# Reordering the hand-written instruction list of a fused Mamba and mixture-of-experts kernel

## The chip, the core and the metric

The kernel runs on one core of one Trainium2 chip. The metric is the time of one execution in device microseconds (us); lower is better. One execution was also recorded by the hardware profiler, and its profile and trace are what the sections below read.

## What is computed

Two layers on x of 32 sequences x 256 tokens x 128 channels, all in fp32: a Mamba block and a mixture of experts, each behind a layer norm and added to x.

```python
# Mamba block, on xn = layernorm(x):  d_inner 256, d_state 16, dt_rank 8
xi, res = split(xn @ W_in)
u       = silu(causal_conv4(xi) + conv_b)
dr, B, C = split(u @ W_x)
delta   = softplus(dr @ W_dt + b_dt)
h_t     = exp(delta_t * A) * h_(t-1) + delta_t * B_t * u_t     # for 256 channels x 16 states
y_t     = sum over states of h_t * C_t, + u_t * D
x       = x + (y * silu(res)) @ W_out
# mixture of experts, on xn = layernorm(x): 8 experts, the 2 best per token
cw      = softmax over the two best of xn @ gate_w.T, zero elsewhere
x       = x + sum over e of cw[:, e] * (silu(xn @ w1[e].T) @ w2[e].T)
```

## The kernel before

**Tiling.** The 32 sequences are cut into 17 tiles (0 to 16): the first and the last hold one sequence, the fifteen others two. A tile's tokens stand as columns, its channels as the 128 partitions, in two chunks c. The 16 states of a chunk are taken in groups, so that every scan covers 128 x 1024 elements: four states at a time for a one-sequence tile (8 scans in all), two for the others (16). That makes 256 scans.

**The pieces.** The work is cut into small named pieces, each of which issues a few instructions. A word such as `1:sc3` means piece sc3 of tile 1. In the order in which a tile needs them:

- `ldx` (line L373) loads x; `st1*`, `sa1`, `rs1`, `ap1` are the layer norm (statistics on DVE L538, the power on POOL L554 to L557, the scaling on ACT L563); `tr1`, `hi1`, `nl1`, `lo1` transpose it on PE and split it into a high and a low part on ACT (L614, L624).
- `cv*` is the convolution with W_in folded in, on PE (L635); `u*` its silu (L649); `wx` the product pd with W_x (L658); `rh`, `sb`, `nr`, `rl` its evacuations on ACT (L685, L671, L695); `bcd` stores the B and C rows as bc in DRAM (L677); `gp*`, `gs*` are the gate; `zz`, `sp*` are delta (softplus, L739).
- For each scan k: `rb` and `rc` load B and C rows of bc, broadcast over all partitions (L778, 512 KB each, four buffers each); `dk` computes da = exp(delta A) on ACT (L760, nine buffers); `in` the product db = (delta u) B on DVE (L812); `sc` the scan h on DVE (L819, three buffers for h); `cm` the product h C on POOL (L830); `ys` adds it to y on PE (L834). A row is kept for two scans where the second chunk takes it up. `du`, `dp` (L793, L799) prepare delta u; in tile 0 `dq` does (L807).
- `yc`, `yz`, `yt`, `ye` gate and transpose y, `ldr` loads x once more, `px` and `op` add W_out's product on PE; `st2*` to `lo2` are the second norm.
- `gt`, `sc`, `r0` to `r4`, `rx`, `rw0` to `rw4` rank the experts. For each expert e: `wi` (two halves, three matmuls each, L1079), `si` their silu on ACT (L1092), `wo` on PE (L1100), `as` scales by cw on ACT (L1112), `aa` adds on POOL (L1118); `sto` stores the tile (L1141).

Before all that, pieces of tile 0 prepare weights: `lw`, `lc`, `ldk`, `ldp`, `ldd`, `ldo`, `ldg`, `l10`, `l11`, `ld2` load them (`ld2` is w2, 1 MB, L465), `pm`, `pt` make constants, `km`, `kh`, `kl` fold W_in into the convolution and split it, `ka` makes A, `kdt`, `kwr`, `kw`, `kgt`, `kdg` split or spread the others. In tile 0, `pb0` and `pc0` make the first B rows on PE and ACT instead of by a transfer.

**The order.** Nothing is scheduled by a compiler. One string, ORDER, lists all 3827 words, and the kernel issues them as they stand; each engine's queue, and the transfer queue SP's, takes its own instructions in that order, and waits where an operand or a buffer isn't ready:

```python
with tc.manual_schedule():
    for word in ORDER.split():
        i, n = word.split(":")
        pieces[n](int(i))
```

Two more things depend on the order. ACT holds one set of functions at a time, and a piece asks for its own (exp for `dk`, `ka`, `rx`; silu for `u`, `gs`, `si`; softplus for `sp`), so the order sets how many table loads (L530) there are:

```python
def need(which):
    if table[0] != which:
        nc.scalar.preload_act_table_set(SETS[which])
    table[0] = which
```

And a tile takes a buffer of its pool at the place in the order where its word stands, so a load waits for the last reader of the buffer that is free there.

Of the kernel before, what the change touches and what calls it, by code (L numbers as in the profile page):

```python
# [47 lines left out]
0:pm 0:ldx 0:lw0 0:lc0 0:lc1 0:ldk 0:lw1 1:ldx 0:ldg 0:st10 0:st11 0:l11 0:sa1 0:ldd 0:rs1 0:ldp 0:km0 0:ap1  # L48
3:ldx 0:tr1 0:l10 0:km1 0:hi1 0:nl1 0:kh1 0:lo1 0:kl1 0:kh0 0:cv1 0:kl0 1:st10 1:st12 1:st13 0:ka 1:st11 1:sa1
1:rs1 0:cv0 0:u1 1:ap1 0:kdt 2:ldx 1:tr1 0:u0 0:kwr 0:wx 0:gp0 0:sb 3:st10 0:rh 0:bcd 1:hi1 0:nr 0:ldo 0:rl  # L50
1:nl1 0:gs0 0:zz 1:lo1 0:pb0 0:kw0 0:sp0 1:cv0 0:pc0 0:rb1 0:rc0 0:rc1 2:st10 0:rb2 0:dq0 0:rb3 2:st13 0:in0
0:rc2 0:rc7 0:ld2 0:dk0 0:kw1 1:cv1 0:dk1 0:sc0 0:dk5 2:st12 0:cm0 0:in1 0:dk2 2:st11 2:sa1 0:sc1 0:dk4 0:kdg
0:rc3 2:rs1 0:ys0 0:dk3 0:in2 0:cm1 0:dk6 0:sc2 0:in3 0:cm2 1:u1 1:u0 3:st11 0:sc3 2:ap1 1:wx 0:ys1 0:dq1 1:rh
0:in6 1:sb 1:bcd 0:ys2 0:sc6 1:nr 1:gp0 1:gs0 1:rl 0:in4 1:zz 0:cm3 1:gp1 1:rb1 3:st13 0:sc4 1:rb5 1:sp0 0:ldr
1:sp1 0:pt 0:ys3 1:du0 0:in5 0:yc0 0:cm4 1:rb4 0:sc5 0:dk7 0:yz0 0:ys4 0:in7 0:kgt 1:dk3 0:cm6 0:yt0 1:dk0
1:rb0 0:sc7 2:tr1 1:rc1 0:px 1:dp0 0:cm5 1:rc0 2:hi1 1:dk6 1:dk2 0:cm7 0:ys5 1:in0 0:ys6 1:rb6 1:sc0 2:nl1
0:ys7 0:yc1 1:dk1 0:yz1 1:in1 1:du1 2:lo1 3:st12 1:rb2 0:ye0 3:sa1 0:yt1 4:ldx 1:cm0 1:sc1 0:ye1 1:rc2 1:dk4
0:op 1:dk8 1:cm1 2:gp0 0:st20 0:st21 1:dk5 1:ys0 1:in2 1:dk9 0:sa2 1:rb3 1:sc2 0:rs2 0:x2 1:rc4 1:rc3 1:rc5
0:ap2 0:tr2 1:in5 1:cm2 1:ys1 0:hi2 0:nl2 1:sc5 0:lo2 0:gt 0:wi50 1:gs1 2:gs0 0:sc 2:cv0 1:in3 0:si50 0:r3
1:rb7 1:sc3 0:r4 1:rc7 1:dk11 1:ys2 1:dk7 1:in4 1:cm3 0:rx 1:dk10 0:r0 1:sc4 1:dk12 3:rs1 1:rc6 1:ys3 0:wi40  # L60
1:in6 2:cv1 1:cm4 2:u0 4:st10 1:sc6 1:cm5 1:rc13 1:ys4 2:u1 0:r1 0:si40 2:wx 1:in7 3:ap1 0:wi00 0:r2 0:wi70
1:sc7 0:rw0 0:wi20 0:si70 1:ldr 0:rw4 1:ys5 2:rh 1:cm6 0:si00 1:dp1 2:gp1 0:si20 2:sb 0:wi41 1:in8 0:wi60
0:si60 1:cm7 2:gs1 3:tr1 1:rb15 1:sc8 0:wi71 2:nr 1:ys6 2:rl 0:si41 0:si71 0:wi11 3:hi1 1:in9 1:cm8 3:nl1
0:wi30 0:wi10 0:rw1 0:si10 1:rb13 1:sc9 0:si11 2:bcd 0:wi51 1:ys7 0:wi21 0:si21 1:in10 1:cm9 0:si51 0:wo7
0:si30 1:yc0 0:rw2 3:lo1 2:zz 1:rb12 1:sc10 1:rc11 0:wo2 1:ys8 1:dk15 1:in11 1:cm10 2:rb3 1:sc11 1:rc12 2:sp0
0:rw3 0:wo4 1:yz0 0:as2 2:sp1 0:wi01 0:as4 1:in12 1:ys9 0:aa4 0:wi31 4:st11 1:rb14 1:ys10 1:cm11 1:sc12 1:rc14
0:si01 1:yt0 0:wo0 1:dk13 1:in13 2:rc0 1:ys11 1:ye0 1:cm12 4:st12 2:rb0 1:dk14 1:sc13 2:dk2 1:rc15 1:ys12
1:in14 1:cm13 2:dk6 2:rb4 2:dk4 1:sc14 0:aa2 1:ys13 2:dk3 2:du0 1:in15 2:dk0 3:cv0 1:cm14 2:rb1 0:as7 1:sc15
2:rc3 2:dp0 0:as0 2:dk1 2:rc1 2:in0 1:cm15 2:dk7 4:st13 2:rb5 2:sc0 0:wi61 3:gp1 0:si31 1:ys14 2:in1 2:cm0
1:ys15 2:dk5 2:rb2 2:sc1 3:cv1 2:rc2 2:dk9 2:rc4 1:yc1 2:dk8 2:in3 2:cm1 2:ys0 4:sa1 2:sc3 2:du1 2:rc5 3:u1  # L70
2:rb6 3:u0 1:px 1:yz1 0:si61 2:in2 3:wx 5:ldx 2:cm3 1:yt1 2:sc2 2:ys1 1:ye1 3:rh 3:gp0 3:sb 3:gs0 2:rc6 2:in4
# [36 lines left out]
4:cm13 5:rb0 4:sc14 5:rc1 3:as1 4:ys12 3:as2 3:aa1 4:ys13 4:in15 6:lo1 5:dk1 4:px 4:cm14 7:st11 5:rb3 4:sc15
3:wo5 5:rc0 5:dp0 5:dk0 3:wo0 3:as5 5:in0 4:cm15 5:dk4 5:rb2 5:sc0 4:ys14 5:dk7 3:aa5 4:ys15 3:wo4 4:yc1 7:sa1
# [1117 lines left out]
```

## Time and profile before

| | |
|---|---|
| median of 3 runs | 1052.45 us (1048.10 to 1054.97) |
| profiled execution | 1053.02 us, of which its span is 1051.3 us |
| mean granted TensorE clock | 0.982 |
| read from HBM, written | 217.28 MB, 5.24 MB (212 GB/s over the span) |

Busy time of each engine in the three stretches that the first and the last scan bound (us; windows of the profile):

| stretch | length | PE | DVE | ACT | POOL |
|---|---|---|---|---|---|
| start to first scan, 0 to 28.16 | 28.16 | 18.61 | 12.32 | 17.85 | 6.45 |
| first to last scan, 28.16 to 1012.26 | 984.10 | 910.92 | 941.92 | 901.86 | 884.51 |
| last scan to end, 1012.26 to 1051.30 | 39.04 | 34.71 | 2.55 | 26.86 | 23.07 |

How to read the profile lines below. Engines: PE is the matmul engine, PEld its weight loads, DVE the vector engine, ACT the scalar engine, POOL the GpSimd engine, SP the queue that issues transfers. A group line gives the code line, engine, operation, output<-inputs with shapes and count | busy us, mean ns of one | idle us of the engine just before them, and what ended most of it. A timeline line gives start us, duration us, and the instruction, and in brackets the idle time before it and who ended it. A wait line gives total us, times, longest. A window line gives the stretch, then busy us and instructions for PE, PEld, DVE, ACT, POOL, then the granted clock of PE, the DMA share and GB/s. The slices are 40 equal parts of the span, each digit the busy share in tenths.

### The profile page before, as it was taken

The numbers are of one execution on the slowest core, as the hardware profiler recorded it, in microseconds if no ns is written. First come the engines' busy times: TensorE is split into PE (matmuls) and PEld (weight loads), VectorE is DVE, ScalarE is ACT, GpSimd is POOL, SyncE is SP. The second block draws the span as 40 slices with busy tenths as digits, with TensorE's granted clock in tenths as the row PEclk, the third lists the DMA queues.
The fourth block names the chain that finished last, engine by engine and source line by source line (L and its number), as shares of the span: only waits on it lengthen the run. The fifth ranks groups of instructions, "written<-read, shape, count | busy, mean of one in ns | idle before, by whom it ended". The sixth has DMA issues, their size and how long they took to land.

```text
span 1051.3 us, 18971 instructions
## 1 busy us (share of the span) xinstructions
PE 964.2 (92%) x6757; PEld 843.7 (80%) x6757; DVE 956.8 (91%) x903; ACT 946.6 (90%) x1914; POOL 914.0 (87%) x688
## 2 busy tenths in 40 slices
PE   6578789999999999999999999999899999999998
PEld 4467667979888887978888887978778888887898
DVE  3999999999999999999999999999999999999950
ACT  6867989999899998999999898989989998899977
POOL 2577788979989999989999999998989999899975
PEclk9879999999999999999999999999999999999999
DMA  5565848658486775758577684848667584776500
GB/s 180 192 225 173 282 149 281 238 183 275 159 249 220 243 268 192 265 165 283 194 263 247 197 284 140 285 176 282 231 215 252 191 286 159 256 233 201 172 11 17
DMA packets 86095, 223.75 MB, mean 213 GB/s; under 512 B 8049, under 2 KB 35313, under 8 KB 85873
## 3 DMA queue, kind: packets, MB, share of 16 engines
q1 hardware_dynamic: 86000, 222.55, 63.7%
q8 instruction: 53, 0.87, 0.3%
q14 instruction: 42, 0.34, 0.1%
HBM read 217.28 MB, written 5.24 MB: 212 GB/s over the span
## 4 chain that ended last, share of the span: by engine, by line
PE 34%; ACT 29%; DVE 18%; POOL 10%; issue 7%; DMA 1%; SPq 0%; DVEq 0%; POOLq 0%; ACTq 0%
DVE h L819 11%; ACT da L760 11%; PE pf L1079 10%; PE y L834 7%; POOL h L830 6%; PE pe L1100 6%; DVE db L812 6%; ACT L530 5%; ACT so L1112 4%; ACT hs L1092 3%; PE pc L635 3%; POOL x L1118 2%; PE po L941 1%; PE pg L703 1%; PE pd L658 1%
## 5 line engine op out<-in xcount | busy, mean ns | idle before, releaser
L830 POOL TENSOR_TENSOR h<-h,rc 128x1024 f32<-128x1024 f32 x256 | 607.1, 2381 | 62.1 <-DVE h L819 52.2
L819 DVE TENSOR_TENSOR_SCAN h<-da,db 128x1024 f32<-128x1024 f32 x256 | 584.5, 2283 | 25.5 <-PE y L834 7.8
L760 ACT ACTIVATE da<-de,a_sb 128x510 f32<-128x510 f32 (+1 forms) x544 | 341.1, 714 | 0.9 <-DVE h L819 0.4
L812 DVE TENSOR_TENSOR db<-du,rb 128x1024 f32<-128x1024 f32 x256 | 314.9, 1230 | 10.5 <-ACT du L799 2.3
L834 PE MATMUL y<-ident,h 128*128 128x128 f32 x2048 | 268.6, 277 | 16.4 <-POOL h L830 16.0
L834 PEld LDWEIGHTS y<-ident,h 128*128 128x128 f32 x2048 | 237.0, 143 | 37.9 <-POOL h L830 25.7
L1100 PE MATMUL pe<-w_sb,hs 128*128 128x128 f32 x2048 | 249.3, 277 | 9.4 <-ACT so L1112 3.0
L1100 PEld LDWEIGHTS pe<-w_sb,hs 128*128 128x128 f32 x2048 | 237.8, 192 | 16.7 <-ACT so L1112 4.9
L1079 PE MATMUL pf<-xt,w_r 128*128 128x512 f32 (+1 forms) x816 | 215.8, 398 | 14.1 <-DVE rank L1028 6.4
L1079 PEld LDWEIGHTS pf<-xt,w_r 128*128 128x128 f32 x816 | 138.3, 189 | 53.8 <-ACT hs L1092 15.5
L1092 ACT ACTIVATE hs<-pf 128x512 f32<-128x512 f32 (+1 forms) x272 | 143.8, 577 | 40.6 <-PE pf L1079 37.4
L1118 POOL TENSOR_TENSOR x<-x,so 128x512 f32<-128x512 f32 (+1 forms) x136 | 166.0, 1221 | 13.3 <-ACT so L1112 12.3
L1112 ACT ACTIVATE so<-pe,cw 128x128 f32<-128x128 f32 x512 | 147.4, 390 | 4.2 <-PE pe L1100 2.0
L530 ACT ACT_TABLE_LOAD x101 | 129.6, 1283 | 1.8
L635 PE MATMUL pc<-xt_r,wc_r 128*128 128x512 f32 (+1 forms) x408 | 101.0, 399 | 2.7 <-ACT xt_r L624 0.9
L635 PEld LDWEIGHTS pc<-xt_r,wc_r 128*128 128x128 f32 x408 | 74.6, 198 | 18.6 <-issue 2.0
L911 POOL TENSOR_TENSOR g<-yt,g 128x512 f32<-128x512 f32 (+1 forms) x34 | 41.4, 1218 | 7.5 <-ACT yt L904 7.5
L793 POOL TENSOR_TENSOR dus<-de,u 128x512 f32<-128x512 f32 (+1 forms) x32 | 40.3, 1260 | 6.6 <-ACT de L739 6.6
L851 PE MATMUL y<-dg_sb,u 128*128 128x128 f32 x256 | 35.7, 282 | 8.3 <-ACT yt L904 4.2
L851 PEld LDWEIGHTS y<-dg_sb,u 128*128 128x128 f32 x256 | 32.7, 194 | 12.9 <-ACT yt L904 7.5
L941 PEld LDWEIGHTS po<-wo_sb,yt 128*128 128x128 f32 x256 | 31.2, 195 | 4.2 <-issue 2.9
L941 PE MATMUL po<-wo_sb,yt 128*128 128x128 f32 x256 | 32.7, 280 | 0.8 <-ACT yt L922 0.8
(95 smaller groups left out, 705.6 us busy)
## 6 DMA issues: line engine op xcount, KB each, us to landing
rc<-bc SPq DMA_DIRECT2D x205, 512.0 KB, 5.1
rb<-bc SPq DMA_DIRECT2D x187, 512.0 KB, 4.7
xa<-in_x SPq DMA_DIRECT2D x15, 256.0 KB, 4.5
xc<-in_x SPq DMA_DIRECT2D x15, 256.0 KB, 5.5
out<-x SPq DMA_DIRECT2D x15, 256.0 KB, 5.0
w1h<-in_w_t SPq DMA_DIRECT2D x2, 512.0 KB, 5.0
bc<-s SPq DMA_DIRECT2D x32, 32.0 KB, 2.2
w_sb<-in_w_t SPq DMA_DIRECT2D x1, 1024.0 KB, 10.8
```

Of the source, the lines that this page charges most:

```text
L530: nc.scalar.preload_act_table_set(SETS[which])
L635: nc.tensor.matmul(pcv, wc_r[a][:, j, c * P : (c + 1) * P], xt1_r[b][:, : nb[i], o + j : o + j + L], start=(k == 0), stop=(k == 3 * KC - 1),)
L760: nc.scalar.activation(da[:, m, :, 1:], de[:, :, 1:], AF.Exp, scale=a_sb[:, c, n : n + 1])
L812: nc.vector.tensor_mul(db, d["du"].unsqueeze(1).to_broadcast([P, gs[i], tok[i]]), rows["b", i, k])
L819: nc.vector.tensor_tensor_scan(flat(h), da_of(i, k), flat(d["db"]), 0.0, ALU.mult, ALU.add,)
L830: nc.gpsimd.tensor_tensor(h, h, rows["c", i, k], ALU.mult)
L834: nc.tensor.matmul(y[:, q, :], src[:, q * P : (q + 1) * P], ident, is_transpose=True, start=False, stop=last, skip_group_check=True,)
L1079: nc.tensor.matmul(pf, w1_r[a][:, e, f * P : (f + 1) * P], d["xt"][b], start=(k == 0), stop=(k == 2),)
L1092: nc.scalar.activation(d["hs", e][:, f, :], d["pf", e, f], AF.Silu)
L1100: nc.tensor.matmul(pe[:, q, :], hs[:, f, q * P : (q + 1) * P], w2_sb[:, e, f, :], start=(f == 0), stop=(f == FC - 1),)
L1112: nc.scalar.activation(so[:, q, :], d["pe", e][:, q, :], AF.Copy, scale=d["cw"][:, q, e : e + 1])
L1118: nc.gpsimd.tensor_tensor(x2, x2, st[i]["so", e], ALU.add)
```

## The change

Only the string ORDER changes. It was found by a search that took the transfers of the ramp to be as long as they were measured. The words are the same 3827, each once; the code of every piece is the same (the string is one line shorter, so all code lines have a number less by one). The sequence of the 256 scans and of their `in` differs by two exchanges of neighbours (`1:sc0` and `1:sc1`, `3:sc0` and `3:sc1`), that of the `ys` not at all, that of the `cm` at 8 places, that of the `dk` at 185. Against the scans, words move by 11 at most; the largest moves are among `aa`, `rc`, `st`, `sto`, `ldr`. The number of table loads, which follows from the order, goes from 101 to 105. Of the string's 236 lines (235 after), the beginning and the end:

```diff
 ORDER = """
-0:pm 0:ldx 0:lw0 0:lc0 0:lc1 0:ldk 0:lw1 1:ldx 0:ldg 0:st10 0:st11 0:l11 0:sa1 0:ldd 0:rs1 0:ldp 0:km0 0:ap1
-3:ldx 0:tr1 0:l10 0:km1 0:hi1 0:nl1 0:kh1 0:lo1 0:kl1 0:kh0 0:cv1 0:kl0 1:st10 1:st12 1:st13 0:ka 1:st11 1:sa1
-1:rs1 0:cv0 0:u1 1:ap1 0:kdt 2:ldx 1:tr1 0:u0 0:kwr 0:wx 0:gp0 0:sb 3:st10 0:rh 0:bcd 1:hi1 0:nr 0:ldo 0:rl
-1:nl1 0:gs0 0:zz 1:lo1 0:pb0 0:kw0 0:sp0 1:cv0 0:pc0 0:rb1 0:rc0 0:rc1 2:st10 0:rb2 0:dq0 0:rb3 2:st13 0:in0
-0:rc2 0:rc7 0:ld2 0:dk0 0:kw1 1:cv1 0:dk1 0:sc0 0:dk5 2:st12 0:cm0 0:in1 0:dk2 2:st11 2:sa1 0:sc1 0:dk4 0:kdg
-0:rc3 2:rs1 0:ys0 0:dk3 0:in2 0:cm1 0:dk6 0:sc2 0:in3 0:cm2 1:u1 1:u0 3:st11 0:sc3 2:ap1 1:wx 0:ys1 0:dq1 1:rh
-0:in6 1:sb 1:bcd 0:ys2 0:sc6 1:nr 1:gp0 1:gs0 1:rl 0:in4 1:zz 0:cm3 1:gp1 1:rb1 3:st13 0:sc4 1:rb5 1:sp0 0:ldr
-1:sp1 0:pt 0:ys3 1:du0 0:in5 0:yc0 0:cm4 1:rb4 0:sc5 0:dk7 0:yz0 0:ys4 0:in7 0:kgt 1:dk3 0:cm6 0:yt0 1:dk0
-1:rb0 0:sc7 2:tr1 1:rc1 0:px 1:dp0 0:cm5 1:rc0 2:hi1 1:dk6 1:dk2 0:cm7 0:ys5 1:in0 0:ys6 1:rb6 1:sc0 2:nl1
-0:ys7 0:yc1 1:dk1 0:yz1 1:in1 1:du1 2:lo1 3:st12 1:rb2 0:ye0 3:sa1 0:yt1 4:ldx 1:cm0 1:sc1 0:ye1 1:rc2 1:dk4
-0:op 1:dk8 1:cm1 2:gp0 0:st20 0:st21 1:dk5 1:ys0 1:in2 1:dk9 0:sa2 1:rb3 1:sc2 0:rs2 0:x2 1:rc4 1:rc3 1:rc5
-0:ap2 0:tr2 1:in5 1:cm2 1:ys1 0:hi2 0:nl2 1:sc5 0:lo2 0:gt 0:wi50 1:gs1 2:gs0 0:sc 2:cv0 1:in3 0:si50 0:r3
+0:ldx 0:lw0 0:lc0 0:lc1 1:ldx 0:ldp 0:ldd 0:ldk 0:st10 0:st11 0:sa1 0:km1 0:km0 1:st10 1:st13 0:pm 0:rs1 0:ap1
+2:ldx 0:ldo 0:l11 0:lw1 0:ldg 0:l10 0:tr1 0:kh1 0:hi1 0:kh0 0:kl1 0:kl0 0:kdt 1:st12 0:nl1 0:lo1 0:cv1 0:ka
+0:cv0 0:u1 1:st11 2:st10 1:sa1 2:st12 0:kwr 2:st11 2:st13 2:sa1 0:kw0 0:kw1 1:rs1 1:ap1 3:ldx 1:tr1 0:u0 0:wx
+0:gp0 0:rh 0:sb 0:bcd 0:ld2 0:rc3 1:hi1 0:nr 0:rl 0:gs0 1:nl1 0:zz 0:pb0 0:sp0 1:lo1 0:pc0 0:rb1 0:rb2 0:rc2
+0:rc0 0:rb3 0:rc1 0:dq0 0:in0 0:dk0 0:sc0 0:in1 3:st10 1:cv0 1:cv1 0:dk1 0:dk2 0:dk5 0:sc1 0:in2 0:sc2 0:dk3
+0:dk4 0:dk6 1:u1 0:in3 0:cm0 0:kdg 0:ys0 1:u0 1:gp0 0:pt 2:rs1 0:cm1 0:ys1 0:cm2 1:wx 0:dq1 0:sc3 1:gs0 1:sb
+1:rh 0:cm3 0:in6 1:nr 1:rl 3:st12 0:sc6 1:bcd 1:rc1 1:rb1 1:gp1 0:ys2 1:zz 0:ys3 0:in4 1:rb5 0:sc4 0:in5 1:sp0
+1:sp1 1:du0 2:ap1 0:yc0 0:ldr 1:rb4 0:cm4 0:rc7 0:yz0 3:st11 0:sc5 0:in7 0:cm5 1:rb0 0:cm6 1:rc0 0:ys4 0:yt0
+0:px 0:ys5 0:ys6 2:tr1 1:dk2 0:dk7 0:sc7 1:dk4 1:dp0 0:ye0 1:dk1 1:dk5 1:dk0 1:in1 0:kgt 0:cm7 1:rb6 1:sc1
+0:ys7 1:in0 1:sc0 3:st13 2:hi1 1:dk6 0:yc1 1:rb2 3:sa1 1:du1 0:yz1 1:cm0 0:yt1 2:nl1 1:dk10 0:ye1 2:lo1 0:op
+0:x2 2:gp0 0:st20 0:st21 0:sa2 0:rs2 1:cm1 1:in2 1:dk9 0:ap2 1:dk8 1:ys0 1:rc2 4:ldx 1:rb3 1:sc2 1:cm2 1:in5
+0:tr2 0:hi2 4:st10 1:sc5 1:dk3 0:nl2 0:lo2 1:ys1 0:gt 0:wi50 0:sc 1:in3 0:r3 3:rs1 0:r4 1:sc3 1:gs1 2:cv1
...
-16:rc2 15:ys15 15:px 16:in1 14:aa0 15:yc1 16:dk2 14:wo4 15:yz1 16:sc1 14:as1 16:cm0 14:as5 15:yt1 16:in2
-15:ye1 16:dk3 15:op 16:cm1 16:rc7 16:sc2 16:dk6 14:wi21 15:st20 16:ys0 16:cm2 15:st21 15:st22 15:st23 16:in3
-16:gp0 14:si21 15:sa2 16:ys1 16:sc3 16:dp1 15:rs2 15:x2 14:wo2 15:ap2 16:in6 16:cm3 16:ys2 15:tr2 16:sc6
-15:hi2 16:gs0 14:aa1 15:nl2 16:ys3 15:lo2 15:wi10 16:in4 14:as2 14:aa5 15:wi30 15:si10 16:cm6 15:gt 16:sc4
-14:as4 15:si30 15:wi40 15:wi50 15:si40 15:sc 15:r0 15:wi41 15:r1 15:r2 15:wi60 15:si41 15:r3 16:in5 15:rw0
-15:si50 15:wi51 16:cm4 16:yc0 15:wi31 15:si60 16:sc5 15:wi20 15:si31 15:si51 15:wi70 15:r4 15:si20 16:yz0
-16:ys4 14:aa2 16:in7 15:wi00 15:rx 15:rw4 16:sc7 15:wi11 16:cm5 15:wo5 15:si70 15:si00 15:rw1 15:rw2 16:yt0
-15:rw3 16:px 16:cm7 15:as5 16:ys5 15:si11 16:ys6 16:ye0 15:wi01 14:aa4 16:ys7 15:wo1 14:sto 16:yc1 15:si01
-16:yz1 15:aa5 16:yt1 15:wi21 16:ye1 16:op 15:wo0 16:st20 16:x2 16:st21 15:si21 16:sa2 15:as1 16:rs2 15:wi71
-15:as0 15:wo3 16:ap2 15:aa0 15:si71 15:wi61 15:as3 15:aa1 16:tr2 15:wo4 15:si61 15:aa3 16:hi2 16:nl2 15:wo2
-16:lo2 15:as4 16:gt 15:as2 16:wi20 16:sc 16:wi30 16:r3 16:r0 16:si20 16:wi00 16:r1 16:si30 16:wi10 16:r2
-16:si00 16:wi21 16:rw0 16:wi31 15:aa2 16:si21 16:wi60 16:si10 16:wi01 16:si31 16:wi40 16:si01 16:r4 15:wo6
-16:si60 16:si40 16:wi50 16:rx 15:as6 15:wo7 16:rw4 15:aa4 16:rw1 16:rw2 16:rw3 15:aa6 16:wi41 16:wo0 16:si50
-15:as7 16:wo2 16:as0 16:wi70 16:si41 16:wi51 16:aa0 16:si70 16:wi71 16:si51 15:aa7 16:wo4 16:si71 16:as2
-16:wi11 16:wo7 15:sto 16:as4 16:si11 16:aa4 16:wi61 16:wo1 16:as7 16:aa2 16:wo5 16:as1 16:aa7 16:si61 16:wo3
-16:aa1 16:as5 16:wo6 16:aa5 16:as3 16:aa3 16:as6 16:aa6 16:sto
+15:ye0 16:dk5 14:as0 14:aa0 16:dk7 15:yc1 16:in1 14:as5 16:dk2 15:yz1 16:sc1 14:wo4 15:yt1 15:ye1 15:px 16:rc7
+16:rc0 16:cm0 16:cm1 16:rb2 16:in2 16:rc2 13:sto 16:rc3 16:dk3 14:as1 16:sc2 16:gp0 15:op 15:x2 16:dk6 15:st20
+16:cm2 16:ys0 16:ys1 14:wi21 16:in3 15:st23 15:st21 15:st22 15:sa2 16:sc3 15:rs2 14:si21 16:dp1 15:ap2 16:gs0
+16:ys2 14:wo2 16:in6 16:cm3 15:tr2 15:hi2 16:sc6 14:aa1 14:aa5 15:nl2 16:ys3 15:lo2 15:wi30 15:wi10 16:in4
+14:as2 15:gt 16:sc4 16:cm6 15:si10 15:wi40 14:as4 15:si30 16:yc0 15:si40 15:wi41 15:wi50 15:si41 15:si50
+16:in5 15:sc 15:r0 15:r3 15:r1 15:r2 16:yz0 16:cm4 15:r4 14:aa4 15:rw0 15:wi60 15:wi11 15:wi01 15:wi20 16:ys4
+16:sc5 15:si60 15:wi51 15:rx 15:rw4 15:rw1 16:in7 15:rw2 16:sc7 16:cm5 14:aa2 15:rw3 16:cm7 15:si20 15:wi70
+15:si11 15:wi31 15:si51 15:wo5 15:si70 15:wi00 16:ys5 15:si00 16:yt0 16:ys6 15:si31 15:si01 14:sto 16:ys7
+16:yc1 15:as5 16:ye0 16:yz1 15:aa5 15:wo1 16:px 16:yt1 15:wi21 16:ye1 16:op 16:st20 16:st21 16:sa2 16:rs2
+15:wo0 16:x2 15:wi61 15:as1 15:wo3 15:si21 15:as0 16:ap2 16:tr2 15:wi71 15:aa0 15:si61 15:wo4 15:as3 15:aa3
+15:aa1 16:hi2 16:nl2 15:wo2 16:lo2 15:si71 15:as4 16:gt 15:as2 16:wi20 16:sc 16:r0 16:r1 16:si20 16:r2 16:r3
+16:wi00 16:wi30 16:si30 16:wi31 16:wi10 16:wi01 16:rw0 16:r4 16:si00 16:wi60 16:si31 16:si10 16:si01 16:wi40
+16:si60 16:si40 16:rx 16:rw4 15:aa4 16:rw1 16:rw2 16:rw3 15:aa2 16:wi21 15:wo6 16:wi50 16:si21 16:si50 15:as6
+15:aa6 15:wo7 16:wi41 16:wo0 15:as7 16:si41 16:wo2 16:wi70 16:as0 16:si70 16:wi71 16:wo4 16:wi11 16:si71
+16:wi61 15:aa7 16:as2 16:wo7 16:aa0 16:si11 16:wi51 16:as4 15:sto 16:wo1 16:aa2 16:aa4 16:as7 16:aa7 16:si51
+16:wo5 16:si61 16:as1 16:aa1 16:wo3 16:as5 16:wo6 16:aa5 16:as3 16:aa3 16:as6 16:aa6 16:sto
 """
```

## The prediction

> **What bounds the kernel now.** I read the page from the top: busy shares, then the 40 slices, then the groups of the engine that looks fullest.
>
> ```profile
> span 1051.3 us, 18971 instructions
> PE 964.2 (92%) x6757; PEld 843.7 (80%) x6757; DVE 956.8 (91%) x903; ACT 946.6 (90%) x1914; POOL 914.0 (87%) x688
> ...
> PE   6578789999999999999999999999899999999998
> ...
> DVE  3999999999999999999999999999999999999950
> ```
>
> Five queues stand at about 90%, so the average names no bound. The slices do: DVE is full from the second slice to the 38th and then empty, and PE is full at the end. So there are three stretches: a ramp until DVE starts, a DVE stretch, and a tail in which PE works off what is left.
>
> ```profile
> L819 DVE TENSOR_TENSOR_SCAN h<-da,db 128x1024 f32<-128x1024 f32 x256 | 584.5, 2283 | 25.5 <-PE y L834 7.8
> ...
> L812 DVE TENSOR_TENSOR db<-du,rb 128x1024 f32<-128x1024 f32 x256 | 314.9, 1230 | 10.5 <-ACT du L799 2.3
> ...
> L530 ACT ACT_TABLE_LOAD x101 | 129.6, 1283 | 1.8
> ```
>
> The 256 scans and their 256 products db are 899 us of DVE that no order can shorten. The timeline gives the borders. The first scan starts at 28.16:
>
> ```profile
> 14.80 1.66 ACT L563 ACTIVATE xn_a<-xa,mr_a,rs_a 128x128 f32<-128x128 f32 x4 [2.46 <-POOL mr_a L557]
> ...
> 16.36 0.46 ACT L649 ACTIVATE u<-pc,small_sb 128x256 f32<-128x256 f32 x1
> ...
> 24.64 0.44 SPq L465 DMA_DIRECT2D w_sb<-in_w_t  x1
> ...
> 26.34 11.31 ACT L760 ACTIVATE da<-de,a_sb 128x255 f32<-128x255 f32 x28
> ...
> 28.16 2.29 DVE L819 TENSOR_TENSOR_SCAN h<-da,db 128x1024 f32<-128x1024 f32 x1
> ...
> 30.52 2.36 POOL L830 TENSOR_TENSOR h<-h,rc 128x1024 f32<-128x1024 f32 x1 [15.76 <-DVE h L819]
> ```
>
> The last scan runs from 1009.97 to 1012.26. So: ramp 28.2 us, DVE stretch 984.1, tail 39.0. In the DVE stretch, DVE's waits (asked for 28 to 1010 alone) add up to 21.7 us. The two largest among those of the scans:
>
> ```profile
> DVE h L819 <- PE y L834: 7.8, 14, 1.5
> ...
> DVE h L819 <- ACT da L760: 2.9, 6, 0.9
> ```
>
> The first is the wait for one of three h buffers, which PE's y sum frees. In the tail the chain of waits is PE without a gap, from 999.91 to 1046.98:
>
> ```profile
> 1002.72 5.71 PE pf L1079 x24
> ...
> 1043.40 3.58 PE pe L1100 x32
> ```
>
> **The change part by part.** The new order holds the same 3827 words, so no work is added or removed but for table loads, which the code inserts wherever the set changes. DVE's 256 scans keep their sequence but for two swapped neighbours (tiles 1 and 3, k 0 and 1); y sums keep theirs entirely. Counted in scans, words move by up to 11, on average by less than one.
>
> 1. Ramp, weights. Before, SP issued the 1 MB w2 load at 24.64, behind seven rows. Now it stands straight behind the store of bc (19.42), ahead of every row. The windows from 24 to 34 us show 350 to 434 GB/s, so at 400 each row lands about 2.6 us later for it. The second row that DVE needs, rb1, then has 1.05 + 0.52 + 0.52 MB ahead and in it: 5.2 us from 21.0 (first row issue before), plus 2.2 to landing (the row of bc, the smallest store) is 28.4; its db ran at 30.55, so nothing waits. rc0 has three rows more: 3.7 MB, 9.2 us, lands near 32.4; POOL's first h*rc ran at 30.52, so it goes 1.9 us later. Its y sum frees an h buffer that the fourth scan needs at 39.53: 32.4 + 2.4 (h*rc) + 0.75 (dg) + 1.9 (y) = 37.5. Hidden, with 2 us to spare; without that cover it costs up to 1.9.
>
> 2. Ramp, chain. km1 and kh1 now go before km0 and hi1. kh1 waits for the second half of the convolution weights (its product ended at 7.56), so hi1 slips from 6.69 to about 8.2, and the last split lo1 from 8.12 to about 9.5: the convolution starts 1.4 us later. Before, it did not set the end: u0 waited until 16.36 behind the norm of tile 1 (14.80), which waited for POOL, which had waited for the table of A on ACT (10.32). That follows lo1 in both orders, so u0 slips by about 1.2. Against this stands that the split lo1 of tile 1 now goes behind softplus instead of ahead of it (0.58), and that PE no longer sits idle from 13.67 to 15.35, after which its clock read 0.60 and 0.54 and the product pd took 1.97 instead of the 1.08 that twice as many matmuls take at 88.61. Gains bounded by 0.6 + 1.4 = 2.0, loss by 1.4. I take +0.5 for the ramp; its ends are -0.6 and +1.4.
>
> 3. First tile. The norm of tile 2 (1.65 us of ACT) moves from ahead of tile 1's rh and s to behind its softplus. So tile 1's rows are asked for up to 1.65 earlier, but PE now runs y1 ahead of tile 1's pd, which hands back 1 to 2 us (y took 1.9 here at half clock). The 2.9 us of gt split on DVE (55.46 to 58.30) only changes places with two neighbours. I take 0, between -1.65 and +1.65.
>
> 4. Table loads: 101 become 105; the net growth lies in the first 32 scans (18 to 22). 4 x 1.283 = 5.1 us more of ACT. What hides it is ACT's idle time there:
>
> ```profile
> 50.00:75.00 25.00, 15.91 (x83) 13.62 (x82) 23.17 (x24) 17.58 (x33) 19.58 (x15) 0.73 0.62 197
> 75.00:100.00 25.00, 20.84 (x143) 17.44 (x140) 24.26 (x21) 19.05 (x37) 17.61 (x15) 1.00 0.56 196
> 100.00:125.00 25.00, 18.99 (x133) 16.81 (x131) 23.54 (x18) 24.40 (x43) 20.18 (x12) 0.93 0.81 259
> ...
> 1000.00:1025.00 25.00, 25.00 (x174) 22.75 (x174) 12.76 (x17) 18.13 (x45) 18.80 (x19) 1.00 0.04 11
> ```
>
> Fourth busy column: ACT is idle 14.0 of these first 75 us, but only 0.6 of the last 25. da has nine buffers and is computed up to eight scans ahead, so a load that lands in the tight part uses up the lead first. I take 0; the ends are 0 and 5.1. Do the loads cost more than their row says? On the timeline of ACT:
>
> ```profile
> 49.03 0.37 ACT L904 COPY yt<-y 128x256 f32<-128x256 f32 x1
> 49.42 1.28 ACT L530 ACT_TABLE_LOAD   x1
> 50.72 4.16 ACT L760 ACTIVATE da<-de,a_sb 128x255 f32<-128x255 f32 x8
> ```
>
> The gaps on both sides are 0.02 us, so nothing is added here. The Trainium skill says otherwise ("ScalarE: Activation LUTs", What ACT_TABLE_LOAD costs): a switch of set is the same 1283 ns and a drain of some 1380 ns. By that rule, four more would be an estimated 10.6 us, and this change would lean to slower.
>
> 5. Row loads. Many rb and rc words move close to their use (nine rb words now stand in the same scan as their reader, before none). But SP issues a load when its buffer is free. I counted the scans between the last reader of a buffer and the first reader of the row that takes its place: 2 or more for all but two rb before and all but one after, and for every rc. At 3.69 us a scan (period of the timeline) that is 7.4 against medians to landing of 4.7 and 5.1. Cost 0; where the lead falls to one scan, 5.1 - 3.7 = 1.4 each.
>
> 6. The middle, tiles 2 to 14: wi, si, wo, dk shuffled by a few scans. The trace of before can't price it; the bounds are that DVE's 21.7 us of waits all go, or double. I take 0, since the kinds of dependency and the buffers are the same.
>
> 7. Tail. Behind the last scan the new order has one w1 group (three matmuls, 0.71 at 1015.34) and three silus more, and two small steps of the ranking less. But counted from the fifth scan from the end (tile 16, k 3, at 993.70), PE has the same words left in both, and PE is saturated since 999.9. I take 0; ends -0.7 and +0.7.
>
> Sum: +0.5 against the profiled execution's 1053.02 (span 1051.3 and 1.7 around it), which stands 0.57 above the median: 1052.45 + 0.5, so **1053**.
>
> **The rivals.**
> - A, waits in the middle go: if half of the 21.7 us vanish, 1053 - 11 = 1042. For it: they are spread over 42 places that an order can mend. Against: each is short (longest 1.5), whoever is served earlier takes the time from a neighbour in its queue, and the two orders look alike.
> - B, slower: ACT comes late. Place: the scans of tiles 1 and 2, 100 to 125 us, where ACT has 0.6 us to spare. From the point at which the lead of da is used up, each table load delays a scan by its 1.28; all four: 1053 + 5.1 = 1058. Lost leads that aren't made up, at as much again, 1063. Against: 14 us idle just ahead.
> - C, rows late: the w2 load ahead of the rows lands later than worked out, and db of scans 1 to 3 wait: 1053 + 2.6 = 1056.
> - D, the change does nothing: the moves all fall into slack, 1052.5.
>
> **How the numbers follow.** The forecast with D together 0.50, A 0.22, B 0.20, C 0.08. A change under 1% (10.5 us) is about what a measurement of this kernel can't tell from none, its three runs lying from 1048.1 to 1054.97. Faster by over 1% needs more than half of the waits to go: 0.17 (most of A, a little of the unpriced middle). Slower by over 1% needs B at its far end or waits that grow by half: 0.18. Within: 0.65. The likeliest one's own range is 1049 to 1058; for 8 in 10 I take in A and the far side of B: 1039 to 1066.
>
> **What would show it.** The first scan at 28 to 29.5 (2). POOL's first h*rc near 32.4 with a wait on the rc transfer (1). 105 table loads, and DVE's wait for ACT's da still under 5 us (4); if it is above, B. DVE's wait for rows near zero (5). DVE's waits from the first to the last scan near 22 us (6); if they are nearer 11, A. PE gapless in the tail, 39 us from the last scan to the end (7). A first scan past 31 or a tail past 42 would make the prediction wrong at a step that I costed near nothing.

## The result, and the profile after

The change makes the kernel slower. "Old" and "new" order below are the strings before and after; a ratio is of times, to the old order run on the same chip. (A fourth run of the old order moved its median from 1052.45 to the 1050.28 below.)

| | old order | new order |
|---|---|---|
| median (runs) | 1050.28 us (4) | 1069.23 us (4), 1068.03 to 1069.91 |
| ratio, 95% interval | 1 | 1.0158 [1.0132, 1.0184] |
| profiled execution, its span | 1053.02, 1051.3 us | 1069.37, 1067.6 us |
| start to first scan | 28.16 us | 25.84 us |
| first scan to end of the last | 984.10 us | 1001.98 us |
| end of the last scan to end | 39.04 us | 39.78 us |

The three differences, -2.32, +17.88 and +0.74, add up to the 16.3 us between the two spans. So the ramp is shorter, the tail the same, and the middle has lost 18 us. The page of the new order:

```profile
span 1067.6 us, 18979 instructions
...
PE 973.3 (91%) x6757; PEld 851.5 (80%) x6757; DVE 959.0 (90%) x903; ACT 951.8 (89%) x1918; POOL 912.7 (85%) x688
...
PE   6668789999999899999998999999999899999998
...
DVE  4999999999998989998998989999998999999950
...
L818 DVE TENSOR_TENSOR_SCAN h<-da,db 128x1024 f32<-128x1024 f32 x256 | 584.4, 2283 | 29.0 <-PE y L833 9.9
...
L811 DVE TENSOR_TENSOR db<-du,rb 128x1024 f32<-128x1024 f32 x256 | 315.0, 1230 | 12.6 <-ACT du L798 2.7
...
L529 ACT ACT_TABLE_LOAD x105 | 134.7, 1283 | 1.8
```

DVE's two large groups cost what they did (2283 and 1230 ns each). Its row of 9s now has 8s from the 13th slice on: DVE stops there. The windows, for the stretch of the scans and the two that the prediction's cover was read from, show it in numbers (third busy column DVE, fourth ACT):

```profile
25.84:1027.82 1001.98, 921.35 (x6402) 804.73 (x6401) 944.38 (x858) 907.18 (x1806) 886.51 (x632) 0.97 0.65 217
...
50.00:75.00 25.00, 15.50 (x86) 12.75 (x86) 23.81 (x23) 19.03 (x36) 18.77 (x15) 0.77 0.73 231
...
100.00:125.00 25.00, 18.30 (x112) 16.12 (x109) 23.57 (x16) 24.23 (x41) 18.28 (x11) 0.86 0.79 260
```

DVE's busy time in the stretch grows by 2.46 us (944.38 against 941.92), its idle time by 15.4 (57.6 against 42.2). The wait view of DVE from 28 us to the last scan (us in total, times, longest) says for whom:

```profile
DVE st_c L537 <- ACT x L953: 11.6, 4, 4.5
DVE h L818 <- PE y L833: 9.9, 11, 3.7
DVE sc L1005 <- PE psc L994: 5.3, 5, 2.5
DVE h L818 <- POOL h L829: 3.8, 4, 1.8
DVE h L818 <- ACT da L759: 2.9, 3, 1.8
...
DVE db L811 <- DMA rb<-bc: 0.6, 1, 0.6
```

The old order had 2.1 us in the first row and 0.3 in the third:

```profile
DVE st_c L538 <- ACT x L954: 2.1, 3, 0.8
...
DVE sc L1006 <- PE psc L995: 0.3, 1, 0.3
```

Rows of B and table loads (da) are not the loss. The largest wait of all, in the timelines of ACT and DVE at tile 9 (start, duration, in brackets the idle time before it):

```profile
632.60 0.30 DVE L537 BATCH_NORM_STATS2 st_c<-po 128x6 f32<-128x128 f32 x1 [0.25 <-PE po L940]
...
634.04 5.01 ACT L759 ACTIVATE da<-de,a_sb 128x510 f32<-128x510 f32 x8
638.93 0.58 ACT L953 COPY x<-po 128x512 f32<-128x512 f32 x1
...
639.54 0.69 DVE L537 BATCH_NORM_STATS2 st_c<-po 128x6 f32<-128x128 f32 x3 [4.46 <-ACT x L953]
```

The first statistics of po ran at 632.60, so po was complete. The other three begin 0.03 us after ACT's copy of the same po ends, and ACT's queue held 5 us of da in front of that copy. In the string, `9:x2` stands six `dk` words behind `9:st20` and ahead of `9:st21`; in the old order it stood two words behind `9:st20`. In the program as built, the reader of po that stands second in the string waits on a semaphore of the other's engine, whichever it is. Neither needs the other's data.

The start of each scan, new less old, shows where time is lost:

| scan | 0 | 16 | 56 | 128 | 144 | 160 | 208 | 255 |
|---|---|---|---|---|---|---|---|---|
| us | -2.32 | -0.23 | -3.87 | +2.37 | +6.34 | +10.85 | +16.01 | +15.56 |

The new order leads by 3.87 us at scan 56 and loses 19.4 from there. Most of that lead is the old record's ramp, which has two lengths (see "The ramp" below): old_kw0_later, the old order with one word of the ramp moved, is 3.11 us ahead of the same record at scan 56, and 4.91 at scan 255.

### The profile page after: what moved, and what is told of

It reads as the page before. It is cut to its first block, busy times and chain, and to the rows that moved or that the text cites. A ratio compares the mean times of both kernels' runs of the same rounds, so it can differ in the third digit from the quotient of the medians.

```text
span 1067.6 us, 18979 instructions
## 1 busy us (share of the span) xinstructions
PE 973.3 (91%) x6757; PEld 851.5 (80%) x6757; DVE 959.0 (90%) x903; ACT 951.8 (89%) x1918; POOL 912.7 (85%) x688
## 4 chain that ended last, share of the span: by engine, by line
ACT 34%; PE 31%; DVE 20%; POOL 7%; issue 6%; DMA 1%; SPq 0%; POOLq 0%; DVEq 0%; ACTq 0%
DVE h L818 13%; ACT da L759 13%; PE pf L1078 8%; PE pe L1099 7%; ACT L529 6%; PE y L833 6%; DVE db L811 6%; POOL h L829 5%; ACT so L1111 4%; ACT hs L1091 3%; PE pc L634 3%; POOL x L1117 1%; ACT xn_c L562 1%; PE psc L994 1%; PE po L940 1%
## 5 line engine op out<-in xcount | busy, mean ns | idle before, releaser
L818 DVE TENSOR_TENSOR_SCAN h<-da,db 128x1024 f32<-128x1024 f32 x256 | 584.4, 2283 | 29.0 <-PE y L833 9.9
L811 DVE TENSOR_TENSOR db<-du,rb 128x1024 f32<-128x1024 f32 x256 | 315.0, 1230 | 12.6 <-ACT du L798 2.7
L833 PE MATMUL y<-ident,h 128*128 128x128 f32 x2048 | 273.6, 280 | 16.2 <-POOL h L829 16.1
L833 PEld LDWEIGHTS y<-ident,h 128*128 128x128 f32 x2048 | 239.7, 145 | 35.9 <-POOL h L829 24.2
L1099 PEld LDWEIGHTS pe<-w_sb,hs 128*128 128x128 f32 x2048 | 240.5, 193 | 14.6 <-ACT so L1111 6.6
L1091 ACT ACTIVATE hs<-pf 128x512 f32<-128x512 f32 (+1 forms) x272 | 143.9, 576 | 32.8 <-PE pf L1078 28.2
L850 PEld LDWEIGHTS y<-dg_sb,u 128*128 128x128 f32 x256 | 32.4, 193 | 17.4 <-ACT yt L903 10.6
```

The costliest lines, as they stand in the source:

```text
L811: nc.vector.tensor_mul(db, d["du"].unsqueeze(1).to_broadcast([P, gs[i], tok[i]]), rows["b", i, k])
L818: nc.vector.tensor_tensor_scan(flat(h), da_of(i, k), flat(d["db"]), 0.0, ALU.mult, ALU.add,)
L833: nc.tensor.matmul(y[:, q, :], src[:, q * P : (q + 1) * P], ident, is_transpose=True, start=False, stop=last, skip_group_check=True,)
L1091: nc.scalar.activation(d["hs", e][:, f, :], d["pf", e, f], AF.Silu)
L1099: nc.tensor.matmul(pe[:, q, :], hs[:, f, q * P : (q + 1) * P], w2_sb[:, e, f, :], start=(f == 0), stop=(f == FC - 1),)
```

## The experiments

All edits but those of four kernels are moves of words. In each quoted expectation T is the theory and R its rival, with the numbers used there. The theory T1 of the first experiments: DVE (statistics) and ACT (copy) are coupled at po by the order of their words, and whichever stands second waits for all that the other's queue holds.

**The copy moved behind the statistics.** In six tiles, the same move in each:

```diff
-10:dk4 10:dk11 8:as4 10:dk5 10:rb6 10:sc3 10:dk12 10:dk10 10:dk7 9:x2 9:st21 9:st23 9:st22 ... 9:sa2
+10:dk4 10:dk11 8:as4 10:dk5 10:rb6 10:sc3 10:dk12 10:dk10 10:dk7 9:st21 9:st23 9:st22 ... 9:sa2 9:x2
```

> The new order with one kind of word moved: x2 (ACT's copy of po) of tiles 0, 7, 9, 12, 13 and 15 goes behind the tile's sa2, so behind its last st2; DVE's own sequence is untouched. Theory T1 (DVE's statistics st_c stand behind ACT's copy because both read the PSUM tile po and are served in program order, and ACT has da work queued ahead of the copy): the 11.6 us in which DVE waited for ACT x go to under 1 us, at least 9 of them are kept, and the time is 1069 - 10 = 1059 (1057 to 1061). Rival R1 (ACT is simply late there, with da for the next scans queued in front, so that DVE would have stopped a scan later anyway): the st_c wait goes, but DVE's waits for da, y or h grow by as much and the time stays within 3 us of 1069.

Measured: 1.0054 [1.0034, 1.0073], median 1059.44. The wait for ACT x is gone from the list, and 1.0158 - 1.0054 = 1.04%, 10.9 us, is back. T1 holds, R1 falls by the time. But DVE's waits for y rise from 9.9 to 14.3 us in its profile, so not all that went was a gain.

**The reverse, in the old order.** Ten copies moved ahead of statistics (in tile 9, where the copy stood ahead already, it went behind more da); for example

```diff
-4:st22 5:dk9 5:ys1 4:st23 5:in4 ... 4:rs2 5:rc5 4:x2
+4:st22 5:dk9 5:ys1 4:x2 4:st23 5:in4 ... 4:rs2 5:rc5
```

> The old order with x2 moved ahead of the last st2 words in ten tiles (1, 4, 6 to 12, 14), so that ACT's copy of po, behind da work, comes before statistics that DVE has to take; DVE's own sequence is untouched. Theory T1: st_c waits for ACT x of 0.5 to 2 us appear at about half of the ten places, 5 to 10 us in all, and the time is 1055 to 1060. Rival R1 (ACT's position makes no difference to DVE, the waits only change their name): under 2 us, 1050 to 1052.

Measured: 1.0150 [1.0110, 1.0191], as slow as the new order. From the wait view of DVE, and its timeline with ACT's at tile 7:

```profile
DVE st_c L538 <- ACT x L954: 17.0, 12, 2.6
...
512.31 4.01 ACT L760 ACTIVATE da<-de,a_sb 128x510 f32<-128x510 f32 x6
517.10 0.59 ACT L954 COPY x<-po 128x512 f32<-128x512 f32 x1 [0.78 <-DMA out<-x]
...
517.71 0.50 DVE L538 BATCH_NORM_STATS2 st_c<-po 128x6 f32<-128x128 f32 x2 [2.57 <-ACT x L954]
```

The same picture as at tile 9 above: +15 us from ten words. I had expected half as much; all ten places wait (the other two of the 12 waits, 1.3 us, the old order has too). R1 falls here too.

**Is it the shared tile, or something ahead of the copy?** One line, the string untouched:

```diff
-        nc.scalar.copy(x2, d["po"])
+        nc.scalar.copy(x2, ident.unsqueeze(1).to_broadcast([P, nq[i], P]))
```

> The new order word for word, but ACT's copy x2 reads the constant matrix ident instead of po, so that the second residual and the experts' sum start from a constant (the Mamba block's result is left out of them); the statistics st_c still read po. Theory T1 (DVE waits for ACT's copy only because both read the same PSUM tile; its data are not needed by the statistics): DVE's waits for ACT x, 11.6 us, go to 0 though the words stand as before, and the time falls by about 10, to 1059. Rival R6 (st_c needs something that ACT does ahead of the copy): the waits stay, under another name, and the time is 1067 to 1070.

Measured: 0.9992 [0.9977, 1.0006]. Not 10 but 17 us go: the whole loss. So reading the same tile costs more than DVE's own wait for the copy. (The copy no longer waits for PE's po, and po's buffer no longer waits for the copy; these parts aren't told apart.) Part of the rest is the other direction: ACT's copy waits for DVE's statistics. That row is in ACT's wait view from 28 us to the last scan, and not in the old order's. Below it, tile 8 of the new order in the timelines of ACT, PE and DVE:

```profile
ACT x L953 <- DVE st_c L537: 4.2, 2, 2.4
...
571.97 0.59 ACT L953 COPY x<-po 128x512 f32<-128x512 f32 x1 [2.28 <-PE y L833]
...
577.54 0.69 ACT L648 ACTIVATE u<-pc,small_sb 128x512 f32<-128x512 f32 x1
...
578.28 3.58 PE L1099 MATMUL pe<-w_sb,hs 128*128 128x128 f32 x16 [2.46 <-ACT u L648]
...
582.83 2.29 DVE L818 TENSOR_TENSOR_SCAN h<-da,db 128x1024 f32<-128x1024 f32 x1 [3.67 <-PE y L833]
```

Here the copy stands behind the statistics, and ACT waits 2.28 us. The bracket names PE's y; but the last statistics of po ended at 571.89, 0.08 us before the copy, and the built instruction waits for DVE. Behind the copy stand six da, a table load and u; PE's wo waits for u, y stands behind wo, and the scan waits 3.67 us for y.

**Which word to move there.** First PE's, keeping the six moves of x2_behind:

```diff
-7:wo6 9:ys3 9:sc5 ... 9:ys4 9:sc6
+9:ys3 9:sc5 ... 9:ys4 7:wo6 9:sc6
```

> x2_behind with one word more moved: PE's 7:wo6 goes behind two y sums (9:ys3, 9:ys4) that stood behind it. In x2_behind and in the new order PE's wo waits 2.5 us there for ACT's u to free a PSUM buffer, and the scan behind waits 3.8 us for its y sum. Theory T2 (the y sum itself was ready, it only stood behind a waiting word in PE's queue): the 3.8 us wait goes, DVE's waits for PE y fall from 14.3 to about 10.5, the time goes from 1059.4 to 1055.6. Rival R2 (PE is behind at this place whatever stands first, since u is late): the wait for y stays above 2 us and the time is 1058 to 1060.

Measured: 1.0095 [1.0067, 1.0124], not better than x2_behind and rather worse (the intervals just touch). The scan's wait for y at this place goes, and the next short word takes it over: DVE's copy sc of the gate product waits 5.06 us at 585.90. T2 falls; R2 by the cause, since PE was late through u, whatever stood first, though it had named the wait for y and 1058 to 1060. Then the copy, in all 14 tiles where it stood ahead of rs2:

```diff
-8:st21 9:sc4 8:x2 9:dk9 9:dk11 9:dk12 10:u1 7:as7 9:ys2 8:sa2 ... 8:rs2
+8:st21 9:sc4 9:dk9 9:dk11 9:dk12 10:u1 7:as7 9:ys2 8:sa2 ... 8:rs2 8:x2
```

> The new order with x2 directly behind rs2 in all 14 tiles where it stood ahead (x2_behind did six, behind sa2). This also takes away the other direction of the same coupling: where x2 stands behind the st2 words but early, ACT waits for DVE's statistics (2.28 us at 571.97 in tile 8, after which u, PE's wo and the scan at 582.83 are late by as much). Theory T1: DVE's wait for ACT x stays at 0, its waits for PE y fall from the 14.3 us of x2_behind to about 11, and the time from 1059.4 to about 1056.5. Rival R5 (ACT uses the freed time for nothing that DVE waits for): 1058.5 to 1060.5.

Measured: 1.0061 [1.0043, 1.0078], the same as x2_behind; by the time R5 holds. At tile 8 it did what T1 says (u at 572.68 straight behind da and load, wo at 574.45, and the scan waits 0.29 us). But in PE's wait view one row has grown, from 1.6 us in the new order:

```profile
PE pc L634 <- ACT so L1111: 6.0, 4, 2.0
```

The convolution waits for a PSUM buffer. Keeping these words and taking only the shared tile away tells whether the later copy, or the buffer that it holds, is to blame:

```diff
 # x2_behind_all, and
-        nc.scalar.copy(x2, d["po"])
+        nc.scalar.copy(x2, ident.unsqueeze(1).to_broadcast([P, nq[i], P]))
```

> x2_behind_all word for word, but x2 reads the constant matrix ident instead of po (the Mamba block's result is left out of the second residual, as in x2_from_ident). Theory T5 (what x2_behind_all still loses is that the later copy keeps po's PSUM buffer past the next convolution word, which then takes a buffer that is freed later: 6.0 us of waits of PE's pc): those waits go and the time is that of x2_from_ident, 1052 (1051 to 1054). Rival R7 (the later copy itself makes the second norm and the gate late): the time stays at 1058 to 1060.

Measured: 1.0006 [0.9990, 1.0022], and the row of 6.0 us is gone. T5 by the time: it is what the copy does to po, not where the copy stands. (In x2_behind_all the copy still waited 2.5 us for the statistics at one place; this kernel takes that away too.) That pc took another buffer because po's was still held follows from the pool's rule (a buffer is taken at the word's place); the trace names only the buffer's last reader.

**The statistics moved instead**, gathered behind the first of them:

```diff
-9:st20 10:dk4 10:dk11 8:as4 10:dk5 10:rb6 10:sc3 10:dk12 10:dk10 10:dk7 9:x2 9:st21 9:st23 9:st22
+9:st20 9:st21 9:st23 9:st22 10:dk4 10:dk11 8:as4 10:dk5 10:rb6 10:sc3 10:dk12 10:dk10 10:dk7 9:x2
```

> The new order with x2 where it stands, but the four st2 words of a tile gathered: directly behind the first of them, in tiles 0, 12 and 15 directly ahead of x2. So all statistics stand ahead of the copy and are done early, and PSUM buffers are taken as in the new order. Theory T1: neither DVE waits for the copy nor ACT for the statistics, about 13 to 16 of the 17 us come back, 1053 to 1056. Rival R8 (the statistics, taken early, now wait for PE's product po or push the scans behind them): DVE's waits for PE po rise above 6 us and the time is 1058 or more.

Measured: 1.0045 [1.0028, 1.0062], 11.9 us back, with DVE's waits for po at 2.4. That is a little short of T1's 13 to 16, and the most that a repair of the new order by its words gave, though its interval overlaps that of x2_behind. The 0.45% that stays is open; ACT's copy still waits 2.7 us for the statistics.

**The other short word**, DVE's copy sc behind PE's gate product, alone and on top of x2_behind_all:

```diff
-4:gt 5:in7 4:sc 5:sc7
+4:gt 5:in7 5:sc7 4:sc
```

> The new order with DVE's copy sc of the gate product moved behind one more large DVE operation in tiles 0, 3, 4 and 5 (in tile 4 behind 5:sc7, in tile 5 behind 6:sc7). Theory T1 (a short word that stands directly behind PE's gate product makes DVE wait for PE): DVE's 5.3 us of waits for PE psc fall to under 1.5 and the time to 1069 - 4 = 1065. Rival R1 (PE is the late one there; the scan behind it would wait as long for its y sum): the wait moves to the scans, 1068 to 1070.

> x2_behind_all, and DVE's copy sc moved behind one more large DVE operation in tiles 0, 3, 4, 5 and 11. Theory T4 (once DVE isn't stopped elsewhere, the 6.4 us of waits for PE psc are real losses): they fall to about 1 and the time is 3 to 4 us under x2_behind_all, near 1053. Rival R1 (seen in sc_later: of the 5.0 us that psc gave up, the waits for PE y took 3.5): under 2 us.

Measured: 1.0148 [1.0117, 1.0179] and 1.0066 [1.0051, 1.0081], no gain in either that can be told from none. In sc_later the waits for psc fall from 5.3 to 0.3 us and those for y rise from 9.9 to 13.4; in the other, psc falls from the 2.8 that x2_behind_all had left (6.4 is the figure of x2_behind) to 0.6, and y rises from 13.0 to 15.3. R1 both times: these 5 us were not a loss of their own.

**The cross of the two orders**, cut at the 58th scan, where three words differ:

> The new order up to the scan 4:sc1 (the 58th), then the words of the old order that are left, as they stood. At scan 56 the new order was 3.87 us ahead of the old. Theory T1 (the new order is better in the ramp and the first 58 scans, its loss lies in single words of tiles 4 to 14): the lead is kept, 1050.3 - 3.9 = 1046.4 (1045 to 1048). Rival R1 (DVE's lead is given back to the next engine that is nearly full, ACT or PE): 1050 to 1051. Rival R2 (the early part of the new order pushes work into the later part that then goes missing there): above 1053.

> The old order up to about the 58th scan, then the words of the new order that are left, as they stood: the other half of the cross with new_then_old. Theory T1 (the loss of the new order lies in single words of tiles 4 to 14, whatever came before): DVE's large st_c waits for ACT x at tiles 7, 9, 12 and 15 and its waits for psc come back, 10 to 13 us, and the time is that of the new order plus its early lead, 1069 + 3 to 5 = 1072 to 1074. Rival R3 (the loss was a debt from the ramp, for example rows or da displaced by it): 1050 to 1058.

Measured: 0.9972 [0.9954, 0.9991] and 1.0194 [1.0163, 1.0226]. T1 in both by the time: the loss comes with the later words (st_c waits 12.1 us for ACT x again in the second), and the early words keep their lead to the end (scan 255 is 5.14 us ahead of the old profile). new_then_old beats the old order by 0.3%. That these early words are better beyond the ramp isn't shown: 2.66 of the 5.14 us stand at scan 0 already, and old_kw0_later's scan 255 is 4.91 ahead. Two attempts to better it, x2 behind rs2 and the statistics gathered:

> new_then_old with x2 directly behind rs2 in the 11 tiles where it stood ahead. There DVE waits 1.4 us for ACT x in all. Theory T1: that goes, and 1 us of time: 1048.5 against the 1049.5 of new_then_old, 0.996 of the old order. Rival R5: no difference that can be measured, 0.997.

> new_then_old with the st2 words gathered in the same way in all tiles. The coupling costs little there (DVE waits 1.4 us for ACT x), so theory T1 expects 0 to 1.5 us less than new_then_old's 1049.5; rival R8: 1050 to 1052, from waits for po.

Measured: 0.9969 [0.9957, 0.9981], no different from new_then_old, and 1.0008 [0.9994, 1.0022], 0.4% worse. Where the coupling costs 1.4 us, repairing it everywhere has nothing to win and moves other words.

**Four table loads alone, in the old order** (step 4), at two places:

```diff
-        need("exp")
+        need("exp"), (i, k) in ((1, 1), (1, 9)) and (need("silu"), need("exp"))
```

> The old order with four ACT table loads more: where da of scans 1 and 9 of tile 1 are computed, the set is switched to silu and back to exp once each (105 loads, as in the new order, the four in the stretch from 45 to 100 us). Nothing else differs. Theory T0 (the prediction's step 4: nine da buffers cover them): DVE's waits for da stay under 4 us, the time is within 1 us of the old order. Rival B of the prediction: each load delays a scan, +5.1 us by the rows of the profile. By the page on ScalarE of the Trainium skill, with a drain at each switch, an estimated 10.6.

> The old order with four table loads more, as old_4_loads, but where da of scan 12 is computed in tiles 7 and 11 (about 500 and 750 us), ACT being 93% busy there. Theory T6 (a load costs where a chain through ACT, not only da, has no slack; in the early tiles the second norm and the gate product of tile 0 stand right behind): here the lead of da covers them, 0 to 2 us. Rival B (each load costs its 1.28 at least): +5 us or more, as before (+7.2).

Measured: 1.0068 [1.0047, 1.0089] and 1.0075 [1.0055, 1.0096]: 7.2 and 7.9 us, at both places more than the 5.1 that the loads last (the interval of the first, 4.9 to 9.4 us, reaches down to it). T0 and T6 fall; B is right for loads put there, and rather low. In old_4_loads, timelines of ACT and DVE:

```profile
61.38 0.37 ACT L904 COPY yt<-y 128x256 f32<-128x256 f32 x1 [5.00 <-PE y L834]
61.77 2.57 ACT L530 ACT_TABLE_LOAD   x2
64.36 1.33 ACT L760 ACTIVATE da<-de,a_sb 128x510 f32<-128x510 f32 x2
...
65.72 2.29 DVE L819 TENSOR_TENSOR_SCAN h<-da,db 128x1024 f32<-128x1024 f32 x1 [2.47 <-ACT da L760]
...
80.39 0.17 DVE L1006 COPY sc<-psc 128x16 f32<-128x16 f32 x1 [3.56 <-PE psc L995]
```

ACT was idle for 5 us, as the prediction had seen, but in front of a copy that waits for y, and the loads stand behind that copy: the idle time is over when they begin. Scan 16 starts 7.9 us later against the old profile than scan 8 does. Two loads in a row take 2.57, with no gap. The Trainium skill ("ScalarE: Activation LUTs", What ACT_TABLE_LOAD costs) has a drain of some 1380 ns at each switch, which would make the four an estimated 10.6 us; the timeline shows no such pause, and both times measured are below that. The largest wait further on is that of sc, 3.56 us, which the old order hadn't there.

**The ramp** (step 2), one word of the old order moved:

```diff
-0:pb0 0:kw0 0:sp0 1:cv0 0:pc0 0:rb1 0:rc0 0:rc1 2:st10
+0:pb0 0:sp0 1:cv0 0:pc0 0:rb1 0:rc0 0:rc1 2:st10 0:kw0
```

> The old order with one word moved, the split of w1 (kw0, two DVE operations of 0.68 and 1.25 us on SBUF at 12.74) behind 2:st10, so behind 19 us. In the old order POOL's norm of tile 1 ran beside DVE's splits, and its steps took 0.71 (nm_a) and 0.99 (rmd_r); in the new order, with DVE idle beside them, 0.19 and 0.37. Theory T3 (POOL is slowed by DVE's split beside it): nm_a falls from 0.71 to near 0.2, the norm ends 0.5 us or more earlier than 14.77, u0 before 16.0, and the first scan starts 0.4 to 1.8 us before 28.16 (the larger figure if PE's clock stays up for the product pd). Rival R4 (the new ramp is earlier for another reason): nm_a stays at 0.7 and the first scan at 28.1 to 28.3. The time changes by no more than the ramp.

Measured: 0.9990 [0.9969, 1.0010]; nm_a 0.26 us, the norm done at 13.2, the first scan at 25.22. It looks like T3, but the ramp of old_4_loads is word for word the old one, and its first scan starts at 25.25; in old_4_loads_mid at 25.21, in old_x2_early at 28.43, in old_then_new at 28.33. So the old ramp has two lengths by itself, and this run settles nothing about kw0. nm_a took 0.19 us in old_x2_early, whose first scan is late, so a quick nm_a alone doesn't make the ramp short.

## Why the prediction was wrong

Forecast 1053, with 1039 to 1066 for 8 in 10; measured 1069.23. Of its rivals, B had the sign but another place: table loads in tiles 1 and 2, with DVE late for da, for which it waits 2.9 us as before. Its 0.18 for a loss over 1% named "waits that grow by half" too, and that is what came. Its steps, in order:

1. Weights ahead of rows: right in effect. Rows of B cost 0.6 us of waiting. POOL's first h*rc came at 30.95, not 32.4:

```profile
30.95 2.35 POOL L829 TENSOR_TENSOR h<-h,rc 128x1024 f32<-128x1024 f32 x1 [17.05 <-DMA rc<-bc]
```

2. Ramp, +0.5: the wrong sign against the old profile, -2.32. lo1 and the convolution did slip, by 1.1 (worked out: 1.4). But POOL's norm of tile 1, 12.40 to 14.77 in the old profile, ran from 12.14 to 13.89, and PE stayed busy; its granted clock from 16 to 20 us was 1.00, where the old profile had 0.60 and 0.54, and the product pd took 1.08 and not 1.97:

```profile
12.42 0.19 POOL L554 TENSOR_SCALAR nm_a<-mv_a 128x4 f32<-128x4 f32 x1
...
13.93 1.65 ACT L562 ACTIVATE xn_a<-xa,mr_a,rs_a 128x128 f32<-128x128 f32 x4 [0.78 <-POOL mr_a L556]
...
15.99 1.08 PE L657 MATMUL pd<-u,wx_sb 128*64 128x256 f32 x4
...
25.84 2.29 DVE L818 TENSOR_TENSOR_SCAN h<-da,db 128x1024 f32<-128x1024 f32 x1 [1.78 <-ACT da L759]
```

The old ramp had been read from one record that caught its longer form. In the three records of the long form (28.2 to 28.4) POOL's rmd_r took 0.99 us and PE's clock from 18 to 20 us was 0.50 to 0.54; in the two of the short one (25.2) 0.37 us and 1.00. What decides between them isn't shown. The 12 records of the new ramp lie between 25.5 and 26.2: against the short form the +0.5 is about right, and what the new order gains is to be rid of the 28.
3. First tile, 0 (ends 1.65 either way): from scan 0 to scan 16 the new order lost 2.1, just outside. DVE spent 1.7 of it in one instruction, which is shown at the end.
4. Table loads, 0: right for the new order (105 loads; its scans lose 1.4 us from scan 0 to 32, and 0.15 in new_then_old, with 105 too), but for a wrong reason. The cover that it named, "ACT's idle time there", is no cover: loads put elsewhere cost 1.8 and 2.0 us each.
5. Row loads, 0: right but for the 0.6 us above.
6. **The middle is the step that failed**: "I take 0, since the kinds of dependency and the buffers are the same." They are the same; but what a dependency cost here was set by what stands ahead of its first half in the other engine's queue, and a copy moved by a few words came behind 5 us of da. The range of the unpriced middle was "all go, or double"; the waits did nearly double (21.7 to 39.7 us in the list), and the stretch of the scans grew by 17.88 us, so the bound was right and the 0 taken from it was not. The objection to its rival A, that whoever is served earlier takes the time from a neighbour, is what sc_later shows, and doesn't hold for x2.
7. Tail, 0 (0.7 either way): +0.74. PE runs it without a gap, as before:

```profile
1046.40 3.47 PE pf L1078 x27
1059.74 3.58 PE pe L1099 x32
```

A rule of the Trainium skill bore on step 6 and was not weighed. "PSUM — Partial Sum Buffer" says (Terms) that two engines on one bank and partition quadrant at once are an error, "reads against reads included", and (PSUM bank collisions raise a hardware error) that the compiler back end's scheduler adds a dependency between two such instructions on different engines, ACT against DVE too. The timelines agree as far as they go: wherever the second reader waited for the first, it began 0.03 to 0.08 us after the first had ended, and in no trace do the two overlap. No run here lets them collide.

## What to carry to other kernels

In a hand-written order, look for pairs of instructions on two engines that read the same PSUM tile: here they were ordered by their words, and the second waited for all that stood ahead of the first in its queue. Keep such words together, with no block of long operations between them. Idle time of an engine that works off its queue in order covered nothing that stood behind the wait, and the record of one execution can be of one of two ramps: compare two before costing a step against it.

## What the runs showed of the hardware

The same DVE instruction, 128x256 du<-de,u, took 0.41 us in the old profile, 2.15 in the new and 0.43 in new_then_old:

```profile
41.73 0.41 DVE L807 TENSOR_TENSOR du<-de,u 128x256 f32<-128x256 f32 x1
...
36.74 2.15 DVE L806 TENSOR_TENSOR du<-de,u 128x256 f32<-128x256 f32 x1
...
36.41 0.43 DVE L806 TENSOR_TENSOR du<-de,u 128x256 f32<-128x256 f32 x1
```

In the new order POOL's h*rc had started at 36.24, ahead of it; in new_then_old, with the same words, it started at 36.85, when du was done. POOL's nm_a took 0.71 us beside DVE's w1 split in the old profile, and 0.19 in the new, where DVE was idle. Yet DVE's 256 scans and products db kept 2283 and 1230 ns through all orders, with POOL as busy. By the program, each of these reads one of its two operands from PSUM (db, du), while du<-de,u reads both from SBUF. Which pairs hinder each other was not tried.
